# Attention and local-attention kernel: the finishing of a slot moved into the next slot's first point, more sums by transfer, more key tiles in parts

## The chip, the cores and the metric

The kernel runs on one core of one Trainium2 chip. A core has five engines with queues of their own: TensorE (PE, with its weight loads as PEld), VectorE (DVE), ScalarE (ACT), GpSimd (POOL) and SyncE (SP), which here only issues transfers. Transfers run on 16 DMA engines that all issuers share. The metric is the device time of the core in microseconds (us), as the median of several runs. A profile is one execution recorded by the hardware; its span runs from the first to the last instruction.

## The reference

Two layers work on four images of 64 x 64 pixels with 256 channels, in float32. Layer 0 is full self-attention over the 4096 pixels of an image, with a residual. Layer 1 is a depthwise 3x3 convolution with three outputs a channel, two pointwise layers with a GELU between, a residual, and attention over each pixel's 3x3 neighbours.

```python
# layer 0, x: (4, 4096, 256), q and k have 32 channels
energy = jnp.einsum('bnd,bmd->bnm', q, k)
attn = jax.nn.softmax(energy, axis=-1)
x = gamma * jnp.einsum('bnm,bmc->bnc', attn, v) + inputs
# layer 1
perceived = depthwise_conv3x3(x) + b_perc             # 768 channels
hid = gelu(w_up1 @ perceived + b_up1)                 # 512 channels
h_new = x + w_up2 @ hid + b_up2
return h_new + local_attention_3x3(h_new)             # zero-padded borders
```

## The kernel before

**Slots and points.** Layer 0 is cut into 32 slots of 512 queries (4 images, 8 slots each; slot `s` is block `s % 8` of its image). A slot goes through the 4096 keys of its image in 16 half groups of 256 keys, that is two key tiles of 128 each, counted `n` = 0 to 15 (`G, half = divmod(n, 2)`). The main loop gives one point to each half group. Layer 1 follows the slots at a distance: convolution two slots behind, hidden layer three, local attention five. Its pieces are jobs, hung on points by the lists `jobs`, so that each point has attention work and one piece of layer 1. The tile framework turns what the program says into waits, but each engine takes its instructions in the order of the program text, which is written out by hand. So an instruction that waits holds up all that stands behind it on its engine.

**One point** (main loop from L1246): SyncE issues the loads that are due (keys, values, forms); ScalarE makes the high part of the next half group's weights; TensorE does the energies of the half group after that (`energy`, L400), ScalarE their exponentials into a tile `p` (three buffers); then come the jobs of layer 1, and then `product` (L423), which adds values times weights to the accumulators. After that VectorE does `add_up` for the next half group (L480), and some tap steps of the convolution, as many as the list `share` says for this point.

**Whole and in parts.** A float32 product on TensorE can be made whole (L435, operands in float32), or in parts: the weights are split into a high part `ph` (ScalarE), a low part `pl` and a gap `pg` (VectorE, L502 and L506), the values likewise in forms kept in HBM, and three products in the reduced float32 kind (`F32R`, L458) give two sums in PSUM, which `finish` puts together. Half groups 2, 4 to 14 (`IN_PARTS`) are in parts in all slots but 0, 2 and 31. In "full" slots (25: all but 0, 1, 2, 7, 15, 23 and 31) half groups 3, 5 to 13 (`ONE_IN_PARTS`) have their second tile in parts and their first whole; `oh`, `ol`, `og` (L420, L486, L489) are the parts and `vo` (L326) the forms of that tile, in four rotating buffers `vs`. Half groups 0, 1 and 15 are whole.

**Sums of the weights.** The softmax's denominator needs the sum of all `p`. Of a full slot's half groups, 3 to 13 are sent by POOL as transfers that add (`send`, L470), the odd ones into a tile `sent`, the even ones into a tile of the pair `xc`; VectorE adds 0, 1, 2, 14 and 15 (L504) and then the two sent tiles (L513), the two halves (L514), and makes sums by 32 (`partial_sums`, L524).

**The slot's end.** `finish` (L545) stands after point 15. TensorE folds the partial sums over partitions (`dps`, L551); VectorE takes reciprocals (L554), spreads them (L540, L543), adds the two accumulators (L567) after ScalarE has scaled the gap sum (L561), scales by the reciprocal (L569) and adds the result to the image in SBUF (L575). Four accumulator banks are all there are, so product 0 of the next slot waits for L567 or L569. TensorE's other work shares two banks `m`, in turn.

**Slots with projections.** In slots 0, 7, 15 and 23 `project_v` (L334) makes the values of an image and packs them with their forms in HBM.

Of the kernel before, what the change touches and what calls it, by code (L numbers as in the profile page):

```python
# [9 lines left out]
F32 = mybir.dt.float32  # L10
F32R = mybir.dt.float32r
# [5 lines left out]
P = 128  # L17
# [35 lines left out]
ONE_IN_PARTS = (3, 5, 7, 9, 11, 13)  # L53
BY_DMA = (ONE_IN_PARTS, (4, 6, 8, 10, 12))
# [6 lines left out]
def attention_then_perception_kernel(  # L61
# [37 lines left out]
    def unshifted():  # L99
# [107 lines left out]
        queries, keys, values, forms, staged = {}, {}, {}, {}, {}  # L207
# [7 lines left out]
        packed_o = tc.dram_tile([P, NSLOT, 2, C], F32, name="packed_o")  # L215
# [10 lines left out]
        def one_in_parts(s, n):  # L226
            return full(s) and n in ONE_IN_PARTS
# [96 lines left out]
        def load_one(s, n):  # L324
            forms[s, n] = tile_of([P, NB], "vs", f"vo_{s}_{n}", 4)
            nc.sync.dma_start(  # L326
                out=forms[s, n].rearrange("p (f c) -> p f c", c=C),
                in_=packed_o[:, block(s, n // 2)],
            )
# [4 lines left out]
        def project_v(s, pair, tag="m"):  # L334
# [11 lines left out]
            split, one = n in IN_PARTS, n in ONE_IN_PARTS  # L346
            h = packed_h[:, s, bass.ts(pair, 2 * C)].rearrange("p (t c) -> p t c", c=C)
            if not split or s < NBLK or s >= NSLOT - NBLK:
# [11 lines left out]
                if not split:  # L360
                    tiles = slice(0, 1 if one else 2)
                    nc.gpsimd.dma_start(out=h[:, tiles], in_=v[:, tiles])
            if split:
                high = fresh(f"vh_{s}_{pair}")
                both = tile_of([P, 2, NB], "sent", f"vlg_{s}_{pair}")
                both = both.rearrange("p f (t c) -> p f t c", c=C)
                to = h, packed_f[:, s].rearrange("p f (t c) -> p f t c", c=C)
            elif one:
                high = fresh(f"vh_{s}_{pair}")[:, 0:1]
                both = fresh(f"vlg_{s}_{pair}").rearrange("p f (t c) -> p f t c", c=C)  # L370
                of = of[:, 1:2]
                to = h[:, 1:2], packed_o[:, s].rearrange("p f (t c) -> p f t c", c=C)
            else:
                return
            low, gap = both[:, 0], both[:, 1]
# [5 lines left out]
            for at, part in zip(to, (high, both)):  # L381
                nc.gpsimd.dma_start(out=at, in_=part)

# [10 lines left out]
        weights, highs, lows, gaps, sent = {}, {}, {}, {}, {}  # L394
        sums, accs, lsums, lrdens = {}, {}, {}, {}
        parts_, inverses, turneds = {}, {}, {}
# [20 lines left out]
        def high_one(s, n):  # L417
            high = tile_of([P, NB], "vs", f"oh_{s}_{n}", 4)
            p = weights[s, n // 2, n % 2]
            nc.scalar.activation(high.bitcast(F32R), p[:, 1, :], AF.Identity, scale=BELOW)  # L420
            highs[s, n] = high

        def product(s, G, half):  # L423
            p = weights[s, G, half]
            first = G == 0 and half == 0
            if first:
                n = 2 * CH if in_two_sums(s) else CH
                accs[s] = [bank("acc", f"acc_{s}_{c}") for c in range(n)]
            v = values[s, G][:, 2 * half : 2 * half + 2]
            last = G == NG - 1 and half == 1  # L430
            if not in_parts(s, G, half):
                one = one_in_parts(s, 2 * G + half)
                for i in range(1 if one else 2):
                    for c in range(CH):
                        nc.tensor.matmul(  # L435
                            accs[s][c], lhsT=v[:, i, bass.ts(c, P)], rhs=p[:, i, :],
                            start=(first and i == 0), stop=(last and i == 1),
                        )
                if one:
                    at = s, 2 * G + half  # L440
                    f = forms.pop(at)
                    for w, to, x in (
                        (v[:, 1], 0, highs[at]), (f[:, :C], 0, lows[at]), (f[:, C:], CH, gaps[at])
                    ):
                        for c in range(CH):
                            nc.tensor.matmul(  # L446
                                accs[s][to + c], lhsT=w[:, bass.ts(c, P)].bitcast(F32R),
                                rhs=x.bitcast(F32R), start=False, stop=False,
                            )
                return  # L450
            f = forms.pop((s, G, half))
            n = IN_PARTS.index(2 * G + half)
            for part, (w, to, x) in enumerate((
                (v, 0, highs[s, G, half]), (f[:, :2], 0, lows[s, G, half]), (f[:, 2:], CH, gaps[s, G, half])
            )):
                for i in range(2):
                    for c in range(CH):
                        nc.tensor.matmul(  # L458
                            accs[s][to + c], lhsT=w[:, i, bass.ts(c, P)].bitcast(F32R),
                            rhs=x[:, i, :].bitcast(F32R),  # L460
                            start=(to > 0 and n == 0 and i == 0),
                            stop=(to > 0 and n == len(IN_PARTS) - 1 and i == 1),
                        )

        def by_dma(s, n):
            if n in BY_DMA[1]:
                return full(s)
            return 0 < s < NSLOT - 1 and (s < 2 or s % NBLK < NBLK - 1) and n in BY_DMA[0]

        def send(s, n):  # L470
            p = weights[s, n // 2, n % 2]
            even = 1 - n % 2
            if n == BY_DMA[even][0]:
# [6 lines left out]
        def add_up(s, G, half):  # L480

            n = 2 * G + half
            if one_in_parts(s, n):
                low, gap = (tile_of([P, NB], "vs", f"o{x}_{s}_{n}", 4) for x in "lg")
                high = highs[s, n]
                nc.vector.tensor_tensor(  # L486
                    low.bitcast(F32R), weights[s, G, half][:, 1, :], high, ALU.subtract
                )
                nc.vector.scalar_tensor_tensor(  # L489
                    gap.bitcast(F32R), low, -SPLIT, high, ALU.mult, ALU.add  # L490
                )
                lows[s, n], gaps[s, n] = low, gap
            p = weights[s, G, half]
            if G == 0 and half == 0:
                sums[s] = tile_of([P, 2, NB], "den", f"den_{s}")
                return
            den = sums[s]
            before = weights[s, 0, 0] if (G, half) == (0, 1) else den
# [4 lines left out]
            if not by_dma(s, n):  # L503
                nc.vector.tensor_tensor(den, before, p, ALU.add)  # L504
# [5 lines left out]
            if G == NG - 1 and half == 1:  # L510
                for even in range(2):
                    if (s, even) in sent:
                        nc.vector.tensor_tensor(den, den, sent.pop((s, even)), ALU.add)  # L513
# [24 lines left out]
        def on_all(values, turned, out):  # L538

            nc.vector.tensor_copy(  # L540
# [3 lines left out]

        def finish(s, parts=((0, RB),)):  # L545

            acc = accs.pop(s)
# [11 lines left out]
            os = [tile_of([P, NB], "o", f"o_{s}_{c}", 2) for c in range(CH)]  # L559
            for o, gap in zip(os, acc[CH:]):  # L560
# [1241 lines left out]
```

## Time and profile before

| what | us |
|---|---|
| median of 3 runs (3247.27 to 3250.21) | 3248.11 |
| the profiled execution's own time | 3249.86 |
| its span | 3248.1 |
| PE busy / DVE busy / ACT busy / POOL busy | 3218.2 / 2866.3 / 1449.8 / 724.1 |
| a late full slot, from fold to fold | 94.4 to 95.2 |

The chain of work that ended last puts 75% of the span on PE and 17% on DVE. The 16 DMA engines moved 190 GB/s in the mean.

How to read it: a group of instructions is named by its line in the kernel, its engine and operation, and the tiles out<-in. Matmuls are pipelined and the ends of their records are modelled, so a record of 592 ns can follow the one before it after 430; what a stretch of PE costs is read from start to start. An f32 matmul has two records, one of the reduced kind has one. A wait is put down to what ended last before it. Busy time is not the same as being the limit: what counts is which wait ends last in a stretch.

### The profile page before, as it was taken

The page shows a single profiled execution, that of the slowest core. Times are in us where ns is not written, and L with a number is a line of the kernel's source. Part 1 is how long each engine was busy: PE and PEld are TensorE (multiplying, and loading weights), DVE is VectorE, ACT ScalarE, POOL GpSimd, SP SyncE. Part 2 cuts the span into 40 slices and gives each one's busy share as a digit, 9 for nine tenths or more (in the row PEclk, how much of TensorE's full clock was granted, in tenths as well). Part 3 has the DMA queues.
Part 4 walks back from the last instruction along what each step waited for, and adds up shares of the span by engine and source line. Part 5 has one row for each costly group of instructions (what it writes and reads, how often), then busy time and mean ns, then how long its engine had stood idle before and what let it go on. Part 6 is the DMA issues. An engine that isn't in the chain of part 4 may idle for free.

```text
span 3248.1 us, 37927 instructions
## 1 busy us (share of the span) xinstructions
PE 3218.2 (99%) x12286; PEld 2223.2 (68%) x12286; DVE 2866.3 (88%) x4380; ACT 1449.8 (45%) x1845; POOL 724.1 (22%) x970
## 2 busy tenths in 40 slices
PE   9999999999999999999999999999999999999998
PEld 5557767766776677676767767776677677667655
DVE  4779899898999999988999999998799999999895
ACT  4434444444444444444444444444444444444331
POOL 3201122221222221222122222211221122222021
PEclk9999999999999999999999999999999999999999
DMA  7767766777667777667766677776777666777100
GB/s 254 222 165 202 194 187 191 202 230 205 196 187 200 211 211 191 186 196 243 205 191 193 184 200 213 208 194 192 253 210 195 190 191 185 201 210 204 49 25 28
DMA packets 289964, 616.58 MB, mean 190 GB/s; under 512 B 97424, under 2 KB 98464, under 8 KB 289632
## 3 DMA queue, kind: packets, MB, share of 16 engines
q1 hardware_dynamic: 228608, 409.47, 40.5%
q0 software_dynamic: 53472, 191.17, 24.8%
q10 hardware_dynamic: 7680, 13.44, 1.1%
q8 instruction: 102, 1.67, 0.2%
q14 instruction: 102, 0.84, 0.1%
HBM read 386.24 MB, written 76.41 MB: 142 GB/s over the span
## 4 chain that ended last, share of the span: by engine, by line
PE 75%; DVE 17%; issue 3%; DMA 2%; ACT 1%; POOL 1%; SPq 0%; ACTq 0%; DVEq 0%; POOLq 0%
PE acc L435 19%; PE acc L458 11%; PE dx L836 5%; PE e L404 5%; DVE perc L666 5%; PE hid_bc L779 5%; PE hid_de L779 4%; PE hid_gf L779 4%; PE acc L446 4%; PE v L339 3%; PE lv L999 3%; PE g L932 3%; PE lo L1133 2%; PE hid_a L779 2%; DVE den L513 2%
## 5 line engine op out<-in xcount | busy, mean ns | idle before, releaser
L666 DVE SCALAR_TENSOR_TENSOR perc<-xp,wb,perc 128x526 f32<-128x526 f32 (+1 forms) x1356 | 941.2, 758 | 1.5 <-ACT perc L662 1.4
L435 PE MATMUL acc<-p,v 128*128 128x512 f32 x1872 | 854.5, 592 | 0.2 <-ACT v L355 0.2
L409 ACT ACTIVATE p<-e 128x1024 f32<-128x1024 f32 x512 | 524.3, 1024 | 546.6 <-PE e L404 490.5
L435 PEld LDWEIGHTS acc<-p,v 128*128 128x128 f32 x1872 | 351.7, 190 | 341.9 <-issue 328.2
L478 POOL DMA_DIRECT2D sent<-p x235 | 201.3, 857 | 1125.6 <-ACT p L409 948.9
L404 PE MATMUL e<-qa,ka 128*128 128x512 f32 x1024 | 368.3, 440 | 2.0 <-ACT p L409 1.1
L414 ACT ACTIVATE ph<-p 128x1024 fp32r<-128x1024 f32 x203 | 214.3, 1056 | 213.2 <-PE acc L458 131.6
L506 DVE SCALAR_TENSOR_TENSOR pg<-pl,ph 128x1024 fp32r<-128x1024 f32 x203 | 267.2, 1316 | 9.0 <-PE e L404 0.5
L502 DVE TENSOR_TENSOR pl<-p,ph 128x1024 fp32r<-128x1024 f32 x203 | 252.2, 1242 | 18.5 <-ACT ph L414 16.8
L458 PE MATMUL acc<-ph,v 128*128 128x512 f32 x812 | 264.0, 447 | 0.2 <-DMA v<-packed_h 0.2
L404 PEld LDWEIGHTS e<-qa,ka 128*128 128x128 f32 x1024 | 189.5, 189 | 88.2 <-issue 45.7
L420 ACT ACTIVATE oh<-p 128x512 fp32r<-128x512 f32 x150 | 94.5, 630 | 317.6 <-PE acc L446 265.4
L836 PE MATMUL dx<-hid,wup 128*128 128x512 f32 x512 | 229.8, 592 | 0.0
L458 PE MATMUL acc<-pl,vf 128*128 128x512 f32 x812 | 223.3, 397 | 0.0
L458 PE MATMUL acc<-pg,vf 128*128 128x512 f32 x812 | 218.7, 391 | 0.9 <-DVE pg L506 0.9
L504 DVE TENSOR_TENSOR den<-den,p 128x1024 f32<-128x1024 f32 x161 | 207.1, 1287 | 5.7 <-ACT p L409 5.3
L1088 POOL TENSOR_TENSOR lsum<-lsum,lp 128x99 f32<-128x99 f32 (+1 forms) x179 | 208.8, 1173 | 11.7
L458 PEld LDWEIGHTS acc<-ph,v 128*128 128x128 f32 x812 | 148.2, 189 | 51.3 <-issue 26.8
L458 PEld LDWEIGHTS acc<-pl,vf 128*128 128x128 f32 x812 | 152.7, 188 | 37.1
L458 PEld LDWEIGHTS acc<-pg,vf 128*128 128x128 f32 x812 | 152.5, 188 | 37.2 <-DVE pg L506 1.4
L802 ACT ACTIVATE hid<-hid,bup 128x512 f32<-128x512 f32 x120 | 80.2, 715 | 211.0 <-DVE hid L786 211.0
L672 DVE TENSOR_TENSOR perc<-perc 128x262 f32<-128x262 f32 x360 | 167.6, 486 | 6.3
(217 smaller groups left out, 4953.3 us busy)
## 6 DMA issues: line engine op xcount, KB each, us to landing
sent<-p POOLq DMA_DIRECT2D x287, 512.0 KB, 6.2
vf<-packed_f SPq DMA_DIRECT2D x203, 512.0 KB, 5.4
v<-packed_h SPq DMA_DIRECT2D x200, 512.0 KB, 4.4
ka<-packed SPq DMA_DIRECT2D x1016, 64.0 KB, 2.8
vo<-packed_o SPq DMA_DIRECT2D x150, 256.0 KB, 4.1
xp<-in_x SPq DMA_DIRECT2D x30, 528.0 KB, 6.1
packed_f<-vlg POOLq DMA_DIRECT2D x28, 512.0 KB, 4.5
xc<-in_x SPq DMA_DIRECT2D x56, 256.0 KB, 3.9
```

The source lines that it names most:

```text
L404: nc.tensor.matmul(e[:, i, :], lhsT=keys[s, G][:, bass.ts(2 * half + i, P)].bitcast(F32R), rhs=queries[s].bitcast(F32R), start=True, stop= ...
L409: nc.scalar.activation(p, e, AF.Exp)
L414: nc.scalar.activation(high.bitcast(F32R), weights[s, G, half], AF.Identity, scale=BELOW)
L435: nc.tensor.matmul(accs[s][c], lhsT=v[:, i, bass.ts(c, P)], rhs=p[:, i, :], start=(first and i == 0), stop=(last and i == 1),)
L458: nc.tensor.matmul(accs[s][to + c], lhsT=w[:, i, bass.ts(c, P)].bitcast(F32R), rhs=x[:, i, :].bitcast(F32R), start=(to > 0 and n == 0 and ...
L502: nc.vector.tensor_tensor(low.bitcast(F32R), p, high, ALU.subtract)
L504: nc.vector.tensor_tensor(den, before, p, ALU.add)
L506: nc.vector.scalar_tensor_tensor(gap.bitcast(F32R), low, -SPLIT, high, ALU.mult, ALU.add)
L666: nc.vector.scalar_tensor_tensor(acc, win, wt, acc, ALU.mult, ALU.add)
L779: nc.tensor.matmul(ps[:, n * C : (n + 1) * C], lhsT=w(j), rhs=rows_of(mixes[s, j][:, kind, :]), start=(j == 0), stop=(j == MULT - 1),)
L836: nc.tensor.matmul(ps, lhsT=wup2[:, d, bass.ts(c, P)], rhs=hids[s][:, d, :], start=(d == 0), stop=(d == NHC - 1),)
L1088: nc.gpsimd.tensor_tensor(to, to, near_ws[block, half][:, t_, of, :], ALU.add)
```

## The change

1. `finish` of a slot in two sums is split. At the slot's end only `evacuate` remains: ScalarE scales the gap sums and VectorE adds the accumulators. The fold, the reciprocal, the scaling and the residual come in the next slot's point 0, behind its jobs and ahead of its product.
2. In full slots half groups 0 to 13 are summed by transfer (2 to 13 in the first slot of an image); VectorE keeps 14 and 15 (and 0 and 1 there).
3. In full slots half groups 1 and 15 get their second tile in parts as well, and 11 and 13 get both tiles. The first tile's forms and parts lie in the four quarters of the buffer `hid`, which the hidden layer uses at points 0 to 7. `low_and_gap` does the VectorE part for each such tile.
4. Two small operations go from VectorE to ScalarE: the spreading of the local denominator's reciprocals and the first scaling of the edge terms.
5. `share` is changed.

```diff
-ONE_IN_PARTS = (3, 5, 7, 9, 11, 13)
-BY_DMA = (ONE_IN_PARTS, (4, 6, 8, 10, 12))
+ONE_IN_PARTS = (1, 3, 5, 7, 9, 11, 13, 15)
+BOTH_IN_PARTS = (11, 13)
+BY_DMA = (3, 5, 7, 9, 11, 13)
+BY_DMA_IF_FULL = tuple(range(14))
...
+        def alone(s, n):
+            return [i for i, ns in enumerate((BOTH_IN_PARTS, ONE_IN_PARTS)) if full(s) and n in ns]
...
+        def load_alone(s, n):
+            for i in alone(s, n):
+                if i:
+                    f, *rest = [tile_of([P, NB], "vs", f"vo_{s}_{n}", 4)] + [None] * 3
+                else:
+                    four = tile_of([P, NHC, NB], "hid", f"vo_{s}_{n}_0")
+                    f, *rest = (four[:, j] for j in range(NHC))
+                forms[s, n, i], rests[s, n, i] = f, rest
+                nc.sync.dma_start(
+                    out=f.rearrange("p (f c) -> p f c", c=C), in_=packed_o[:, block(s, n // 2), i]
+                )
...
+        def high_alone(s, n):
+            for i in alone(s, n):
+                high = rests[s, n, i][0]
+                if high is None:
+                    high = tile_of([P, NB], "vs", f"oh_{s}_{n}", 4)
+                p = weights[s, n // 2, n % 2][:, i, :]
+                nc.scalar.activation(high.bitcast(F32R), p, AF.Identity, scale=BELOW)
+                highs[s, n, i] = high
+
+        def low_and_gap(s, n):
+            for i in alone(s, n):
+                high, (_, low, gap) = highs[s, n, i], rests.pop((s, n, i))
+                if low is None:
+                    low, gap = (tile_of([P, NB], "vs", f"o{x}_{s}_{n}", 4) for x in "lg")
+                p = weights[s, n // 2, n % 2][:, i, :]
+                nc.vector.tensor_tensor(low.bitcast(F32R), p, high, ALU.subtract)
+                nc.vector.scalar_tensor_tensor(
+                    gap.bitcast(F32R), low, -SPLIT, high, ALU.mult, ALU.add
+                )
+                lows[s, n, i], gaps[s, n, i] = low, gap
...
+                apart = alone(s, n)
+                todo += [(v[:, i], 0, p[:, i, :], F32) for i in range(2) if i not in apart]
+                for i in apart:
+                    at = s, n, i
+                    f = forms.pop(at)
+                    todo += [
+                        (v[:, i], 0, highs[at], F32R), (f[:, :C], 0, lows[at], F32R),
+                        (f[:, C:], CH, gaps[at], F32R),
+                    ]
...
         def by_dma(s, n):
-            if n in BY_DMA[1]:
-                return full(s)
-            return 0 < s < NSLOT - 1 and (s < 2 or s % NBLK < NBLK - 1) and n in BY_DMA[0]
+            if full(s):
+                return n in BY_DMA_IF_FULL and (n > 1 or s % NBLK > 0)
+            return 0 < s < NSLOT - 1 and (s < 2 or s % NBLK < NBLK - 1) and n in BY_DMA
...
             if not by_dma(s, n):
-                nc.vector.tensor_tensor(den, before, p, ALU.add)
+                if s in sums:
+                    nc.vector.tensor_tensor(sums[s], sums[s], p, ALU.add)
+                elif s in firsts:
+                    sums[s] = tile_of([P, 2, NB], "den", f"den_{s}")
+                    nc.vector.tensor_tensor(sums[s], firsts.pop(s), p, ALU.add)
+                else:
+                    firsts[s] = p
...
+        def evacuate(s):
+            acc = accs.pop(s)
+            os = [tile_of([P, NB], "o", f"o_{s}_{c}", 2) for c in range(CH)]
+            for o, gap in zip(os, acc[CH:]):
+                nc.scalar.mul(o, gap, -1.0 / (SPLIT + 1.0))
+            if in_two_sums(s):
+                for c, o in enumerate(os):
+                    nc.vector.tensor_tensor(o, acc[c], o, ALU.add)
+                acc = os
+            evacuated[s] = os, acc
...
-            on_all(inverses[at][:, 1, :], turneds[at][:, 1, :], lrdens[s])
+            on_all(inverses[at][:, 1, :], turneds[at][:, 1, :], lrdens[s], nc.scalar.copy)
...
-                nc.vector.tensor_scalar(edge[:, to], of(0), wc[:, 0:1], None, ALU.mult)
+                nc.scalar.mul(edge[:, to], of(0), wc[:, 0:1])
...
-            share = [1, 5, 8, 6, 5, 2, 7, 4, 6, 3, 4, 2, 1, 0, 0, 0]
+            share = [2, 6, 8, 4, 7, 2, 7, 4, 6, 4, 3, 1, 0, 0, 0, 0]
...
-                if one_in_parts(slot, point + 1):
-                    load_one(slot, point + 1)
+                load_alone(slot, point + 1)
...
-                if by_dma(slot, point + 1):
-                    send(slot, point + 1)
+                at = behind[0], 2 * behind[1] + behind[2]
+                if by_dma(*at):
+                    send(*at)
...
                 for do in jobs[point]:
                     do()
+                if slot and point == 0 and in_two_sums(slot - 1):
+                    next(finish(slot - 1))
...
-            if slot < NSLOT - 1:
+            if in_two_sums(slot):
+                evacuate(slot)
+            elif slot < NSLOT - 1:
                 next(finish(slot))
```

## The prediction

> **What bounds the kernel now.** I read the page's busy table first, then the chain and the waits, then one slot's timeline and the windows by slot, and last SyncE's own timeline beside the DMA share.
>
> ```profile
> PE 3218.2 (99%) x12286; PEld 2223.2 (68%) x12286; DVE 2866.3 (88%) x4380; ACT 1449.8 (45%) x1845; POOL 724.1 (22%) x970
> ```
>
> TensorE is in use 99% of the span at a granted clock of 0.999, so what shortens its stream shortens the kernel as long as nothing makes it wait. The PE timeline of slot 10 (start, length, then engine, line, tiles) prices that stream: half group 13 with one tile whole and one in parts, and the end of the slot. The line with "x8" is from the chain: a product of two whole tiles.
>
> ```profile
> 1016.54 0.61 PE L404 MATMUL e<-qa,ka 128*128 128x512 f32 x2
> 1017.00 1.88 PE L435 MATMUL acc<-p,v 128*128 128x512 f32 x4
> 1018.31 1.03 PE L446 MATMUL acc<-oh,v 128*128 128x512 f32 x2
> 1019.18 0.63 PE L446 MATMUL acc<-ol,vo 128*128 128x512 f32 x2
> 1019.65 0.62 PE L446 MATMUL acc<-og,vo 128*128 128x512 f32 x2
> 1020.10 0.62 PE L404 MATMUL e<-qa,ka 128*128 128x512 f32 x2
> ...
> 1028.67 0.41 PE L551 MATMUL dps<-parts,fold 128*128 128x32 f32 x2 [0.85 <-DVE parts L533]
> ```
>
> ```profile
> 1044.31 3.43 PE acc L435 x8
> ```
>
> Records overlap, so I read start to start. Eight records are four f32 matmuls: 3.43/4 = 0.858 us each, 1.715 us a whole tile (two output halves). The steps 0.47 and 0.45 are pairs of reduced matmuls: 0.233 us each, 6 x 0.233 = 1.40 us a tile in parts. Check: 0.466 (energy) + 1.715 + 1.40 = 3.58 against 3.56 from energy to energy.
>
> The fold (`dps`) waits at the slot's end for VectorE. Windows cut at the fold give two kinds of slot (columns: length, then busy of PE, PEld, DVE, ACT, POOL); below them, the wait's total and count.
>
> ```profile
> 933.45:1028.67 95.22, 94.37 (x368) 67.08 (x368) 88.53 (x134) 44.13 (x54) 21.60 (x25) 1.00 0.71 196
> 1123.78:1218.31 94.53, 94.28 (x368) 67.08 (x368) 87.75 (x130) 44.08 (x54) 22.53 (x26) 1.00 0.71 198
> ```
>
> ```profile
> PE dps L551 <- DVE parts L533: 8.6, 20, 1.0
> ```
>
> VectorE is not far behind: 87.75 of 94.5 us. In slot 11 most of its idle time is at the start (2.82 before `hid_de`, 1.44 before `hid_gf`); from there to the fold it runs with gaps of some 0.035 us.
>
> ```profile
> 1041.76 0.69 DVE L786 TENSOR_TENSOR hid<-hid_de,hid 128x512 f32<-128x512 f32 x1 [2.82 <-PE hid_de L779]
> 1044.35 0.69 DVE L786 TENSOR_TENSOR hid<-hid_gf,hid 128x512 f32<-128x512 f32 x1 [1.44 <-PE hid_gf L779]
> ```
>
> Third resource: the DMA engines (window, then the last two columns, share and GB/s), and SyncE's issues at points 12 and 13.
>
> ```profile
> 939.00:945.00 6.00, 6.00 (x21) 3.76 (x20) 4.68 (x8) 1.04 (x2) 0.00 (x0) 1.00 0.02 7
> 997.00:1012.00 15.00, 15.00 (x59) 10.61 (x59) 14.82 (x21) 6.55 (x9) 3.83 (x4) 1.00 1.01 277
> 1012.00:1020.00 8.00, 8.00 (x35) 6.13 (x34) 7.85 (x10) 4.00 (x5) 5.21 (x6) 1.00 0.90 232
> ```
>
> ```profile
> 1011.28 0.32 SPq L326 DMA_DIRECT2D vo<-packed_o  x1
> 1011.65 3.39 SPq L233 DMA_DIRECT2D ka<-packed  x4
> 1015.09 0.46 SPq L312 DMA_DIRECT2D v<-packed_h  x1
> ```
>
> Early in a slot the engines are empty, from point 9 to 13 they are full. The value load at 1015.09 (group 7) lands 5.2 us later, at 1020.26; product 14 needs it at 1020.89. In eight slots (10 to 14, 18, 19, 21) this margin is 0.63, 2.0, 0.76, 1.0, 1.8, 0.89, 2.1 and 1.45 us, mean 1.33. That is the thinnest cover in the kernel.
>
> **What the Trainium skill says.** "FP8 and Floating Point Precision" (TensorE Precision Notes) gives true FP32 four passes and "TensorE: Matmul & The Clock Gate" (Wait — 56ns, not 53.3ns?) 215.7 ns for a warm 512-column matmul: 0.863 and 0.216 us; the trace has 0.858 and 0.233. "DMA: Bandwidth & Descriptors" (Issuing engines are not separate DMA queues) says DMAs of all issuers share 16 engines and interleave: here the key loads issued from 1011.65 landed around 1018, just after POOL's 512 KB sum landed. "SBUF — State Buffer" (SBUF: two separate sides) says a VectorE operation with two SBUF inputs and a GpSimd operation that reads SBUF lock each other out: `og` took 1.34 us at 1015.04 beside `lsum` on POOL, 0.722 in the mean.
>
> **The change part by part**, per full slot (25: 3–6, 8–14, 16–22, 24–30).
>
> *Parts.* Four more tiles (half groups 1, 15, and the second tile of 11, 13): 4 x (1.715 - 1.40) = 1.26 us less PE; 25 x 1.26 = **-31.5**. The PE records are the same kinds in the same places, so I take this as certain where the operands are there in time.
>
> *Fold.* It moves behind the hidden products and `lv` of the next point 0, 0.47 + 3.9 + 1.73 = 6.1 us of PE later; its wait of 8.6 us in all is then covered: **-8.6**. What takes its place: product 0 needs the accumulators, whose two sums (L567, 0.67 each) now stand right behind the partial sums; and the fold's "m" bank needs the `hid_bc` addition (0.69). By my count VectorE ends the partial sums 2.2 to 3.3 us after product 15 and the two sums 1.4 later, against 6.3 when product 0 starts: no stall, 1.6 us to spare. Scaling and residual cost the same on VectorE, 5 us, in place of the idle 2.82 and 1.44.
>
> *VectorE.* Added: four times 0.682 + 0.722 (L486, L489) = 5.62. Removed: three sums (3 x 1.287 = 3.86), the copy for `lrden` (L540, 0.424) and two edge scalings (L971, 0.45), both to ScalarE. Net +0.9: 88.6 busy of 93.0. Slots 8, 16, 24 lose one sum instead of three: near 92.5 of 93.4, so they gain little; I charge 0.7 each, **+2**. Shares move three tap steps (0.76 or 0.49 each) ahead of point 10, which pays for most of the new work at 11, 13 and 15. Adding up in order, `og` of 13's second tile comes 0.3 to 0.5 us before the PE wants it, `pg` of 14 0.3 to 1.3; the lock with POOL can take that.
>
> *ScalarE.* 4 x 0.63 + 0.6 + 0.45 = 3.6 on 44. The edge scaling waits for VectorE's `h`; behind it stand point 8's `oh` and exponential, which wait for product 7 and an energy anyway: nothing. ScalarE's new high parts at 11 and 13 stand before an exponential that is due a point later: nothing; uncovered, 0.63 each.
>
> *Sums by transfer.* 22 x 3 + 3 = 69 more issues on POOL (0.857 us) of 512 KB. The page has 24.8% of 16 engines for 191 MB: 2.2 us of all engines each. They fall at points 15 to 2, where the share is 0.02 to 0.7, and hold a `p` buffer (three) until landed, about 6 us of the three points that there are: nothing. The first waits for VectorE's last sum; behind it on POOL stands only watching.
>
> *Loads.* 100 more `vo` of 256 KB; at 40.5% for 409 MB each is 0.84 us of all 16 engines. Those of 1 and 15 have room. Those of 11 and 13 (first tile) enter SyncE's queue ahead of the keys and values of points 12 and 14, where the engines are full: 1.7 us more, of which 1012–1020 can absorb some 0.8. So group 7's values land 0.8 to 1.7 us later, I take 1.2, and are wanted 0.3 to 0.6 earlier because products 11 and 13 are shorter: 1.65. Over the eight margins max(0, 1.65 - margin) averages 0.44; at the low end (1.1) 0.14, at the high end (2.3) 0.97. With up to 0.1 for VectorE's thin places in the same stretch, which overlap: 0.5 x 22 = **+11** (3 to 24). If it were covered: 0.
>
> *Projections* (slots 0, 7, 15, 23) make more parts on engines with over 20 us idle a slot: nothing, at most +2.
>
> Sum: 3248.1 - 31.5 - 8.6 + 2 + 11 = **3221** on the profiled span. That execution took 3249.86, 1.8 around the span; the median of the runs is 3248.11, so the same difference puts the median at 3221 too.
>
> **Rivals.** (a) *Covered*: the late loads fit, as the early slots' do, and margins hold: 3248.1 - 40.1 = 3208. For it: five of eight margins are 1.0 or more, and `vo` of 11's first tile waits for no late reader, so it may go out early. Against: share 1.01. (b) *The DMA backlog takes most*: the 1.7 us add up with the keys of point 14 (1.7 us of cover, gone when products shorten) to a stall of 1 to 1.7 us: 22 x 1.35 = +30 for +11: 3240, between 3233 and 3254. (c) *VectorE becomes the bound* (slower): if its 4.3 us at `hid_de`/`hid_gf` do not shrink, because the moved finish leaves the same order of waits, each slot is the old 94.5 plus 0.9 and another 0.3 of lock, and three slots 2.6 more: 22 x 0.8 (net of the fold's slack) + 3 x 2 = +24: 3272. It decides where less than 2.7 of those 4.3 us is taken up: 88.6 busy and about 2.5 of small gaps leave 1.9 us in 93.0. Against it: at point 0 the finish now stands exactly in that hole. (d) The change doesn't do what it says: excluded for the parts, since TensorE's instructions are written out.
>
> **How the numbers follow.** Forecast 0.50 (own range 3210 to 3233), (a) 0.27, (b) 0.13, (c) 0.08, else 0.02. The range 3204 to 3241 leaves out (c) and part of (b). 0.2% is 6.5 us, about what a measurement of this kernel can tell from no change: faster is below 3241.6. Forecast, (a) and half of (b): 0.83; same 0.07; slower 0.10.
>
> **What would show it.** Full slots near 93.2 to 93.8 us from fold to fold; L551 without idle before it and `hid_de` idle on VectorE below 1 us; `acc<-p,v` from 1872 to 1472 records; new PE idle, if any, on product 14's `ph` released by a load of `v`, or by `ka` at the energy before; DMA share above 0.95 from point 9 to 13. PE idle released by VectorE (`og`, `pg`) at 12 to 14 would say that the order on VectorE is the tighter cover; a fold that still waits would prove me wrong, and so would slots of over 95 us.

## The result, and the profile after

| | before | after |
|---|---|---|
| median, us | 3247.9 | 3203.8 (3203.1 to 3205.3) |
| ratio, 95% interval | | 0.9864 (0.9846 to 0.9881) |
| span of the profiled execution, us | 3248.1 | 3201.4 |
| a late full slot other than 16 and 24, from fold to fold, us | 94.4 to 95.2 | 92.6 to 92.8 (two took 93.0 and 93.1) |

The kernel is 44 us faster; 27 were forecast. First the page's busy table of the kernel after, and the records of whole products in the groups of PE:

```profile
PE 3179.4 (99%) x12486; PEld 2261.7 (71%) x12486; DVE 2903.6 (91%) x4428; ACT 1550.8 (48%) x2068; POOL 759.6 (24%) x1055
...
L481 PE MATMUL acc<-p,v 128*128 128x512 f32 x1472 | 678.9, 596 | 0.2 <-ACT v L363 0.2
```

The whole records fell from 1872 to 1472, as they had to with 100 tiles more in parts. Next the PE timeline of slot 10 of the kernel after: half group 13 with both tiles in parts, and the fold in its new place.

```profile
1007.89 0.61 PE L418 MATMUL e<-qa,ka 128*128 128x512 f32 x2
1008.35 0.62 PE L481 MATMUL acc<-vo,v 128*128 128x512 f32 x2
1008.80 1.07 PE L481 MATMUL acc<-vo 128*128 128x512 f32 x4
1009.71 0.62 PE L481 MATMUL acc<-oh,v 128*128 128x512 f32 x2
...
1011.07 0.64 PE L418 MATMUL e<-qa,ka 128*128 128x512 f32 x2
...
1024.48 0.30 PE L576 MATMUL dps<-parts,fold 128*128 128x32 f32 x2
1024.62 3.68 PE L481 MATMUL acc<-p,v 128*128 128x512 f32 x8
```

From energy to energy the half group takes 3.18 us, where one whole tile and one in parts took 3.56. The fold waits for nothing, and what follows starts 0.14 us after it (0.25 before). The windows of the kernel after: two full slots from fold to fold, then a stretch early in slot 10, 5.3 to 11.3 us after the slot's first energy, where 939 to 945 lies in the kernel before, and the two stretches up to 1.7 us before and from there to 6.3 us after product 12's start in slot 10, which lie as the two shown of before do (length; busy of PE, PEld, DVE, ACT, POOL; granted clock; share of the DMA engines; GB/s).

```profile
931.65:1024.48 92.83, 92.83 (x378) 68.57 (x377) 89.11 (x134) 47.98 (x63) 23.66 (x28) 1.00 0.84 229
1117.19:1209.80 92.61, 92.61 (x378) 68.64 (x377) 88.78 (x132) 47.55 (x61) 24.48 (x29) 1.00 0.85 231
930.90:936.90 6.00, 6.00 (x23) 3.76 (x22) 4.94 (x12) 0.93 (x2) 1.30 (x2) 1.00 0.98 301
988.30:1003.30 15.00, 15.00 (x62) 11.32 (x61) 14.79 (x23) 7.34 (x10) 3.46 (x4) 1.00 1.02 266
1003.30:1011.30 8.00, 8.00 (x38) 6.72 (x37) 7.72 (x9) 4.45 (x6) 5.16 (x6) 1.00 0.91 261
```

PE busy equals the length of the slot: as far as the records show, TensorE never stands there. The added sums fill the early stretch of the DMA engines, which was nearly empty (share 0.98, 0.02 before). The last two stretches are as full as they were (1.01 and 0.90 before), the last with 261 GB/s in place of 232. The chain that ended last is now PE for 94% (75% before). In the waits of the kernel after (engine, what for, us in total, times, longest) little is left in the full slots:

```profile
PE acc L481 <- DVE pg L520: 2.0, 3, 0.8
...
PE e L418 <- DMA ka<-packed: 0.9, 1, 0.9
PE dps L576 <- DVE parts L548: 0.7, 1, 0.7
```

I set the starts of all energies of the two traces side by side; a point is taken from its energy to the next point's. Of the 46.7 us that the span lost, the parts bring -35.2 and the fold -15.1 in the full slots; where a slot follows one with projections another 4.4 go, which no step of the prediction had; new gaps at points 11 to 14 cost +6.1 (2.4 of it in slots 8, 16 and 24, where VectorE is late), and the rest (start, first slots, end) +1.9.

### The profile page after: what moved, and what is told of

Its sections match the earlier page's. It is cut to its first block, busy times and chain, and to the rows that moved or that the text cites. A ratio compares the mean times of both kernels' runs of the same rounds, so it can differ in the third digit from the quotient of the medians.

```text
span 3201.4 us, 39239 instructions
## 1 busy us (share of the span) xinstructions
PE 3179.4 (99%) x12486; PEld 2261.7 (71%) x12486; DVE 2903.6 (91%) x4428; ACT 1550.8 (48%) x2068; POOL 759.6 (24%) x1055
## 4 chain that ended last, share of the span: by engine, by line
PE 94%; DVE 3%; DMA 1%; issue 0%; POOL 0%; ACT 0%; SPq 0%; ACTq 0%; DVEq 0%; POOLq 0%
PE acc L481 46%; PE e L418 7%; PE dx L857 7%; PE hid_de L800 5%; PE hid_gf L800 5%; PE hid_bc L800 5%; PE lv L1020 3%; PE g L953 3%; PE lo L1154 3%; PE v L347 3%; PE s L1061 2%; PE hid_a L800 2%; DVE perc L687 1%; PE qk L272 1%; PE hid L832 1%; DMA vo<-packed_o 0%
## 5 line engine op out<-in xcount | busy, mean ns | idle before, releaser
L481 PE MATMUL acc<-p,v 128*128 128x512 f32 x1472 | 678.9, 596 | 0.2 <-ACT v L363 0.2
L500 POOL DMA_DIRECT2D sent<-p x304 | 258.0, 855 | 1353.6 <-ACT p L423 823.0
L481 PEld LDWEIGHTS acc<-p,v 128*128 128x128 f32 x1472 | 275.1, 190 | 267.9 <-issue 257.6
L418 PE MATMUL e<-qa,ka 128*128 128x512 f32 x1024 | 357.1, 430 | 5.3 <-ACT p L423 1.5
L520 DVE SCALAR_TENSOR_TENSOR pg<-pl,ph 128x1024 fp32r<-128x1024 f32 x203 | 253.3, 1248 | 11.9 <-DVE pl L510 0.5
L437 ACT ACTIVATE oh<-p 128x512 fp32r<-128x512 f32 x200 | 126.4, 632 | 248.4 <-PE acc L481 83.2
L481 PE MATMUL acc<-oh,v 128*128 128x512 f32 x400 | 184.8, 543 | 0.0
L857 PEld LDWEIGHTS dx<-hid,wup 128*128 128x128 f32 x512 | 96.7, 189 | 98.5 <-issue 93.4
```

What stands on the lines that cost most here:

```text
L418: nc.tensor.matmul(e[:, i, :], lhsT=keys[s, G][:, bass.ts(2 * half + i, P)].bitcast(F32R), rhs=queries[s].bitcast(F32R), start=True, stop= ...
L437: nc.scalar.activation(high.bitcast(F32R), p, AF.Identity, scale=BELOW)
L481: nc.tensor.matmul(accs[s][to + c], lhsT=w[:, bass.ts(c, P)].bitcast(kind), rhs=x.bitcast(kind), start=to not in started[s], stop=last,)
L500: nc.gpsimd.dma_start(out=sent[s, even], in_=p, accum_op=ALU.add)
L520: nc.vector.scalar_tensor_tensor(gap.bitcast(F32R), low, -SPLIT, high, ALU.mult, ALU.add)
L857: nc.tensor.matmul(ps, lhsT=wup2[:, d, bass.ts(c, P)], rhs=hids[s][:, d, :], start=(d == 0), stop=(d == NHC - 1),)
```

## The experiments

All are edits of the kernel after, except where the kernel before is named; its line numbers are other ones. "Before" ran beside them at 3247.5 to 3250.2 us. Intervals are of the ratio to it.

**1. The fold alone, and the fold left behind.** In the first kernel, the kernel before gets only the new place of the fold, scaling and residual; in the second, the kernel after has them back at the slot's end.

```diff
# fold_alone: in before          # fold_back: in after, the reverse
+ if slot and point == 0 and in_two_sums(slot - 1):
+     next(finish(slot - 1))
...
- if slot < NSLOT - 1:
+ if in_two_sums(slot):
+     evacuate(slot)
+ elif slot < NSLOT - 1:
      next(finish(slot))
```

> The kernel before with nothing but the finish split as in the change (accumulators emptied at the slot's end, fold, scaling and residual in the next point 0). Theory S (starts): a fold that waits costs from start to start some 0.28 us more than the idle time that its record shows, and the slots after the projections lose their waits for the shared bank too: -15 in the full slots and -4.4 at the entry to slots 8, 16 and 24, some -19, so 3229 us. Theory R (records, the prediction's count): the 8.6 us of recorded idle time and nothing else, 3239 us.

Measured: 3227.0 us, ratio 0.9934 (0.9917 to 0.9951). 21 us, not 8.6. By points, 15.6 us of it lie at the ends of full slots, 5.2 at the ends of the slots with projections.

> The changed kernel with the whole finish at the slot's end again. In the changed kernel VectorE ends the partial sums 2.0 to 4.1 us after the last product of the slot. Theory V: at the slot's end TensorE would wait for all of that, and a slot is then as long as VectorE's round, about the old 94.5 us plus 0.9 of added work, so 22 slots by 2.5 us and more: about +55, 3258 us (3240 to 3270). Theory A (the parts of the change add up): it gives back only what the move alone brought, +8.6 to +19: 3212 to 3223 us.

Measured: 3295.6 us, ratio 1.0144 (1.0127 to 1.0161): 92 us slower than the kernel after, and 47 slower than the kernel before. Its slot 10 on PE, and its first wait:

```profile
1034.15 0.62 PE L481 MATMUL acc<-og,vo 128*128 128x512 f32 x2
1037.49 0.41 PE L576 MATMUL dps<-parts,fold 128*128 128x32 f32 x2 [2.72 <-DVE parts L548]
...
PE dps L576 <- DVE parts L548: 55.7, 24, 3.9
```

With the other edits in, VectorE ends a slot so late that TensorE stands 2.5 to 2.9 us at the fold in nearly all full slots (4.0 in 8, 16 and 24), where it stood at most 1.2 before (0.16 us added to each recorded wait, see experiment 2). So this edit is worth 21 us alone and 92 among the others. In 14 full slots that stall is the loss; slots 8, 16, 18 to 20 and 24 to 28 get 4.3 to 7.0 us longer, part of it behind the fold, at the next point 0. Why stays open.

**2. Why the wait was worth more than its record.** The kernel before, with the fold reading a constant tile; everything stays where it was.

```diff
+ level = pool.tile([P, 2 * NJ], F32, tag="level", name="level")
+ nc.gpsimd.memset(level, 1.0e25)
...
- given = parts_.pop(s).rearrange("p i j -> p (i j)")[:, :n]
- nc.tensor.matmul(ps, lhsT=fold, rhs=given, start=True, stop=True)
+ parts_.pop(s)
+ nc.tensor.matmul(ps, lhsT=fold, rhs=level[:, :n], start=True, stop=True)
```

> The kernel before, with one thing other: the fold of a slot multiplies a tile that holds a constant in place of VectorE's partial sums, so the denominator is left out of the result, and the fold no longer has anything of VectorE's to wait for. Nothing is moved: inverse, scaling and residual stay at the slot's end, ahead of the next slot's hid products. Theory S (what the move of the fold brought, 21 us, is the wait for VectorE, which is longer than the idle time that the trace records ahead of the fold): 3230 us, from 3227 to 3234, and TensorE goes from the last product of a full slot to the first hid product without a gap beyond the fold's own 0.14 us. Rival R (the recorded idle, 8.6 us, is all of the wait; the rest of the 21 us came from moving scaling and residual behind the next slot's first work): 3239 us.

Measured: 3233.5 us, ratio 0.9957 (0.9940 to 0.9973). The ends of the full slots get 15.5 us shorter, slot by slot the same as with the fold moved (slot 10: 1.11 and 1.12 us). The end of slot 10 on PE, in the kernel before and in this one:

```profile
1024.22 3.59 PE L435 MATMUL acc<-p,v 128*128 128x512 f32 x8
...
1028.92 0.70 PE L404 MATMUL e<-qa,ka 128*128 128x512 f32 x2
```

```profile
1023.46 0.30 PE L554 MATMUL dps<-level,fold 128*128 128x32 f32 x2
1023.60 0.71 PE L407 MATMUL e<-qa,ka 128*128 128x512 f32 x2
```

The last record of the product starts 1.445 us ahead of the fold in the kernel before, 0.429 in this one: 1.016 us of stall, where the record says 0.85, because the modelled end of the product's last record lies 0.16 us past what TensorE needed. And after a stall the next matmul starts 0.244 us after the fold's first, in place of 0.140. Together 1.12 us for a wait recorded as 0.85. Shorter waits lose more in proportion (0.41 us of stall recorded as 0.25 in slot 12), and slot 24's stall of 0.11 has no idle time on record.

The 5.2 us at the slots with projections stay in this kernel. Its waits still have what the kernel after no longer has:

```profile
PE hid_a L782 <- ACT vh L380: 2.5, 3, 1.5
...
PE hid_bc L782 <- ACT hid L795: 1.8, 3, 0.6
```

So these 5.2 us come from moving the finishing, not from the fold's wait; which of its instructions stood in the way was not tried.

**3. The sums of half groups 0 to 2 back on VectorE.**

```diff
-BY_DMA_IF_FULL = tuple(range(14))
+BY_DMA_IF_FULL = tuple(range(3, 14))
```

> The changed kernel with half groups 0 to 2 summed by VectorE again (3 to 13 by transfer): VectorE gets 3.8 us a full slot more, 22 transfers of 512 KB by three fall away. Theory V: VectorE's 88.8 us of 92.6 with some 2.4 us of small gaps has about 1.4 us left, so the slots stretch by about 2.4 us: +50, 3254 us. Rival: its 3.8 us of idle time take all of it: 3204 us, or 1 to 2 us less because the DMA engines have less to do.

Measured: 3247.9 us, ratio 0.9998 (0.9989 to 1.0006): the whole gain is gone. The waits of PE, and a window over about a slot:

```profile
PE acc L481 <- DVE pg L520: 16.3, 24, 1.0
...
PE acc L481 <- DVE og L447: 4.3, 14, 0.3
```

```profile
1104.00:1198.00 94.00, 93.34 (x377) 68.24 (x376) 91.84 (x136) 46.96 (x61) 22.48 (x30) 1.00 0.74 206
```

VectorE, 3 us busier a slot (91.84 of 94.00), now delays products 11 and 14: by points 18.3 and 20.4 us of the 44. Early sums are paid late: VectorE has 2.2 us idle in the whole window.

**4. Parts at 11 and 13, at 1 and 15, and one more at 15.** Three kernels, each one line:

```diff
# both_back
-BOTH_IN_PARTS = (11, 13)
+BOTH_IN_PARTS = ()
# ends_back (and the gap sums end with half group 14 again)
-ONE_IN_PARTS = (1, 3, 5, 7, 9, 11, 13, 15)
+ONE_IN_PARTS = (3, 5, 7, 9, 11, 13)
# both_15
-BOTH_IN_PARTS = (11, 13)
+BOTH_IN_PARTS = (11, 13, 15)
```

> The changed kernel with half groups 11 and 13 as before, one tile whole and one in parts (two loads of 256 KB fewer in each full slot, at points 10 and 12). Theory S: each tile made whole costs 0.38 us from start to start, 25 x 0.76 = +19, and some 4 us of waits at points 11 to 14 go: 3219 us. Theory R (the prediction's terms): 25 x 0.63 = +15.8 and the 11 us charged for late loads go: 3209 us.

Measured: 3218.3 us, ratio 0.9907 (0.9891 to 0.9924), 14.5 us slower. In nearly every full slot point 11 grew by 0.37 and point 13 by 0.39 us, where my step had 0.315 for each.

> The kernel after, with half groups 1 and 15 whole again in the full slots (two full-precision tiles each, as before); 11 and 13 stay with both tiles in parts. Accounting S (what a part brings at these places is the 0.32 us and 0.33 us a slot that the trace showed at points 1 and 15, 16.3 us together, and VectorE's relief brings at most the 2.3 us of late half groups in slots 8, 16 and 24 back): 3204 + 16 - 0 to 2 = 3218 to 3220 us, and the three kinds of edits of the change (fold 21, parts at 11 and 13 14.5, these two 15) then sum to more than the 44 us that the change brought, by what VectorE's fuller queue costs. Rival R (the parts at 1 and 15 are partly paid back by VectorE, which has two more splits and an adding in a slot): 3208 to 3214 us.

Measured: 3226.5 us, ratio 0.9924 (0.9908 to 0.9941), 22.7 us slower, some 20 by the ratios, since "before" took 3250.2 beside it: outside both expectations. Points 1 and 15 grew by 0.33 and 0.32 us, 16 us in all, as expected. The rest lies at point 14, 11 us in the profiled execution, the slowest of its four:

```profile
PE acc L481 <- DMA v<-packed_h: 11.6, 20, 1.0
```

Product 14 waits for its values, though this kernel moves fewer bytes. Experiment 6 takes this up.

> The kernel after, with both tiles of half group 15 in parts in place of one. TensorE has one more product in parts of its eight in 25 slots: 25 x 0.385 = 9.6 us less. VectorE gets one more adding of 1.2 to 1.4 us in a slot, and has 3.8 us idle of 92.6. If VectorE's margin is enough and the added load at point 14 is covered: 3194 us. If VectorE, which in the slots after a projection is already late, sets the end of the slot: 3202 to 3210 us.

Measured: 3214.5 us, ratio 0.9899 (0.9882 to 0.9915), 10.7 us slower than the kernel after. TensorE waits at the fold for the bank that VectorE's addition of the hid products has to free. The wait, and a window of slot 13 from fold to fold, one of the shortest:

```profile
PE dps L576 <- DVE hid L807: 6.0, 10, 1.7
```

```profile
1211.94:1304.36 92.42, 92.42 (x379) 68.94 (x378) 89.97 (x134) 48.14 (x62) 21.90 (x28) 1.00 0.85 230
```

This slot takes 92.42 us, 0.2 less than in the kernel after and not 0.39, and many gain nothing: slots 10, 11, 18 and 19 take 92.9 to 93.2, where they took 92.7 to 92.8. In every full slot point 15 is 0.36 to 0.40 us shorter, and in many the point 0 behind it takes that back; behind the slots with projections it grows by up to 2.9 us.

**5. The transfers: one more, fewer.** The first kernel adds a load ahead of group 7's values, the second leaves 50 loads out.

```diff
# more_load
+ if point == 12 and full(slot):
+     more = tile_of([P, C], "more", f"more_{slot}")
+     nc.sync.dma_start(out=more, in_=packed_o[:, block(slot, 6), 0, 0])
# fewer_loads
+ if i:
      nc.sync.dma_start(out=f..., in_=packed_o[:, block(s, n // 2), i])
...
+ if full(s) and n in BOTH_IN_PARTS:
+     forms[s, n, 0] = forms[s, n, 1]
```

> The kernel after, with one more transfer of 128 KB into a tile of its own at point 12 of each of the 25 full slots, issued on the same queue ahead of the values of half group 14; nobody reads the tile. Theory K (after the change these values land with 0.2 us to spare in the mean and 0.04 us in many slots, so the transfers are just covered and anything more ahead of them is paid at product 14): 128 KB at 213 GB/s are 0.6 us of the transfers' time, of which 0.3 to 0.6 us a slot come to the path: 3212 to 3219 us. Rival C (the transfers are covered by more than the small margin shows, since the margin is that of a queue which is served when the product is near): 3202 to 3206 us.

Measured: 3211.2 us, ratio 0.9888 (0.9871 to 0.9904): 7.4 us for 25 loads, a little under the expected band; points 13 and 14 grew by 4.7 and 3.9 us in its profiled execution.

> The kernel after, but the first tiles of half groups 11 and 13 take the high parts of the second tiles in place of a load of their own, which leaves 50 transfers out and makes the values of these two tiles wrong. All matmuls and all of VectorE's work stay. Theory of the prediction (the transfers that the change adds cost 11 us at products 12 to 14): 3193 us. Theory K (what is paid for them is what the trace shows as new gaps at points 11 to 14 outside the slots that VectorE delays, some 4 us, and the rest is just covered): 3198 to 3202 us. Nothing from them at all: 3204 us.

Measured: 3204.6 us, ratio 0.9869 (0.9852 to 0.9885), no different from the kernel after. So these 50 loads cost nothing that the runs can tell, and one load more in each full slot does cost. Landing and need, in us after product 12's start, mean over the 25 full slots, from the traces:

| | values issued | landed | product 14 starts | margin |
|---|---|---|---|---|
| before | 0.85 | 6.20 | 7.20 | 1.00 |
| after | 1.82 | 6.67 | 6.89 | 0.22 |
| fewer_loads | 1.57 | 6.06 | 6.85 | 0.79 |
| more_load | 2.57 | 7.13 | 7.22 | 0.09 |
| ends_back | 1.77 | 7.32 | 7.40 | 0.08 |
| keys_first (experiment 6) | 1.76 | 6.99 | 7.13 | 0.14 |

The smallest margin that any slot shows is 0.04 us, at which a product that waits for its load starts.

**6. What holds the values' cover.** In the kernel whose ends are whole, the values are issued no later than in the kernel after but fly 0.7 us longer. SyncE's queue shows why. First the kernel after, slot 10 (product 12 starts at 1004.97): the values of group 7, the load for half group 15, the next keys. Then the kernel with whole ends (product 12 at 1009.90).

```profile
1006.99 0.43 SPq L315 DMA_DIRECT2D v<-packed_h  x1
1010.70 0.34 SPq L335 DMA_DIRECT2D vo<-packed_o  x1
1011.10 2.63 SPq L236 DMA_DIRECT2D ka<-packed  x4
```

```profile
1011.68 0.44 SPq L315 DMA_DIRECT2D v<-packed_h  x1
1013.48 1.69 SPq L236 DMA_DIRECT2D ka<-packed  x4
1015.29 0.35 SPq L315 DMA_DIRECT2D v<-packed_h  x1
```

The load for half group 15 waits for a buffer `vs` until 5.7 us after product 12's start, and the keys behind it wait with it. Without it the keys go out 3.6 us after product 12's start, with the next values and forms behind them, and share the engines with the values in flight. The test changes only the order of the queue:

```diff
-                load_alone(slot, point + 1)
+                if point != 14:
+                    load_alone(slot, point + 1)
...
                         spread_queries(slot + 1)
+                if point == 14:
+                    load_alone(slot, point + 1)
```

> The kernel after, with one transfer moved in SyncE's queue: at point 14 the load of half group 15's high and low forms, which waits for a buffer until product 13 is nearly done, stands behind the next keys and values in place of ahead of them. The same transfers, the same bytes. Theory G (the waiting load holds the next keys back until the values of half group 14 have nearly landed; without it the four key loads start 2.3 us earlier, as in the kernel whose half groups 1 and 15 are whole, and share the engines with those values, which land 0.6 us later than the 0.2 us of margin allow): product 14 waits 0.3 to 0.6 us in most of the 25 slots, 3209 to 3218 us. Rival N (that kernel's late values have another cause, such as a different phase of the other queues, and what stands behind the values in the queue doesn't matter to them): 3202 to 3206 us.

Measured: 3212.9 us (3210.0 to 3219.3), ratio 0.9894 (0.9878 to 0.9911), 9 us slower with the same transfers; point 14 grew by 6.7 of the 7.0 us in its profiled execution. Its slot 10 (product 12 at 1003.38) in SyncE's queue, and its first wait:

```profile
1005.35 0.43 SPq L315 DMA_DIRECT2D v<-packed_h  x1
1006.95 1.76 SPq L236 DMA_DIRECT2D ka<-packed  x4
...
PE acc L481 <- DMA v<-packed_h: 6.0, 15, 0.8
```

The values flew 5.50 us there (landed 1010.85), against 4.90 in the kernel after (landed 1011.89); over the 25 full slots the mean is 5.24 against 4.85. The windows over just these flights, of the kernel after and of this one, show the company they had in the last two columns (0.74 of the engines and 215 GB/s; 0.92 and 254):

```profile
1006.99:1011.89 4.90, 4.90 (x23) 3.58 (x21) 4.76 (x6) 2.17 (x4) 4.66 (x6) 1.00 0.74 215
```

```profile
1005.35:1010.85 5.50, 5.01 (x23) 3.58 (x22) 5.36 (x6) 2.77 (x4) 5.19 (x7) 1.00 0.92 254
```

A load that the change added, and that waits, is what keeps the values on time. Whether the keys or the values and forms behind them take most of the room was not separated.

**7. Attempts at more.** With the values ahead of the keys at every even point; with the sum of half group 14 by transfer as well; with both tiles of 15 in parts and the fold behind the first product.

```diff
# values_first: load_values(*after) ahead of load_keys(*ahead)
# sums_15 in the names: and the first tile added to p of half group 15
-BY_DMA_IF_FULL = tuple(range(14))
+BY_DMA_IF_FULL = tuple(range(15))
# later_15: both tiles of 15, and in slots that follow a full one
-                if slot and point == 0 and in_two_sums(slot - 1):   # ahead of product
+                if finishes and behind_it:                          # behind add_up
# later_15_act: and in finish
-            on_all(inverse[:, 0, :], turneds[s][:, 0, :], rden)
+            on_all(inverse[:, 0, :], turneds[s][:, 0, :], rden, copy=nc.scalar.copy)
```

> The kernel after, with the values issued ahead of the keys at every even point, on the same queue; nothing else is moved. Theory G (the values of half group 14 are issued 1.8 us after product 12 starts only because four key loads are issued ahead of them; ahead of these they land 1 us or more earlier, and the keys, wanted two points later, have room): product 14 waits nowhere, and the 2 to 4 us of gaps that the transfers still cost go: 3200 to 3203 us. Rival N (the keys are late instead, or nothing was paid there): 3203 to 3208 us.

Measured: 3232.4 us, ratio 0.9947 (0.9930 to 0.9963), 28.5 slower. The values now land 1.80 us ahead of product 14 in the mean, and the keys are late in their place, since the energy just ahead of product 14 wants them:

```profile
PE e L418 <- DMA ka<-packed: 23.1, 21, 2.5
```

> The kernel after, with both tiles of half group 15 in parts (which took 3214 us by itself), and with the fold, the scaling and the residual moved once more in the 18 slots that follow a full one without projections between: from ahead of the next slot's first product to behind it and behind the splits of half groups 0 and 1. Theory Q (with both tiles of 15 in parts TensorE waits at the fold, since the fold's accumulator bank waits for VectorE's adding of the hid products, which stands behind the slot's last sums; given 3.4 us more, it doesn't wait): the 25 parts at point 15 bring 9.6 us, less the 3 us in slots 8, 16 and 24, and what VectorE, busy 90.2 us of 92.3, then costs elsewhere: 3195 to 3203 us. Rival W (VectorE's work of a slot is what bounds, wherever the fold stands; the wait goes to the splits of later points): 3208 to 3216 us.

Measured: 3217.9 us, ratio 0.9901 (0.9884 to 0.9917), against 0.9899 without the move: the runs do not tell the two apart, and theory Q's gain did not come. The time lies 2 us above rival W's range.

> As the run before it, with one thing more: the copy that spreads the inverse over its square, 0.43 us on VectorE in every slot, is ScalarE's (0.61 us there). Theory Q (VectorE is at its edge, so 0.43 us a slot less of it shows where it still delays products): 1 to 10 us faster than the run before it, 3193 to 3201 us. Rival W': the copy is on no path that matters, within 1 us of the run before it.

Measured: 3224.4 us, ratio 0.9920 (0.9903 to 0.9936), another 6.5 slower, which neither theory had. In both, TensorE's longest wait in total is for ScalarE's exponentials, some 8 us; why stays open.

> As the run before it, with the sum of half group 14 by transfer too, so that VectorE adds 1.25 us less in each full slot. TensorE's work is that of the kernel after. If VectorE still delays products there (slots 8, 16, 24: 2.3 us) and the added transfer is covered: 3198 to 3202 us. If the added transfer of 0.5 MB takes the values' room at product 14, or the denominator waits for it at the slot's end: 3206 to 3216 us.

> The kernel after with both tiles of half group 15 in parts and with the sum of half group 14 by transfer, the queue's order as it was: VectorE's work is that of the kernel after within 0.2 us a slot, TensorE's is 9.6 us less. If VectorE alone made both tiles of 15 cost time: 3192 to 3198 us. If the transfers do it: 3204 to 3216 us.

> As the run before it, with the values ahead of the keys. If both bounds (VectorE's time and the landing at product 14) are what held the parts back, and both are lifted: 3190 to 3197 us, 5 us or more below the run before it where that one pays for transfers. If something else bounds: 3203 us or more.

Measured: 3383.0 us, ratio 1.0411 (1.0394 to 1.0429); 3425.4 us, 1.0541 (1.0523 to 1.0559); 3410.0 us, 1.0497 (1.0480 to 1.0515). All far above what was expected. In the second, the waits of DVE and of PE:

```profile
DVE den L531 <- DMA sent<-p: 185.3, 25, 9.1
```

```profile
PE e L418 <- ACT p L423: 168.7, 25, 8.4
```

The transfer of half group 14 comes last in the chain of the denominator. In slot 10 POOL issued it 10.5 us after product 12's start, in its turn behind other work, and it landed at 19.2, where VectorE's last sums are due from about 11. VectorE waits for it with all that stands behind. These three therefore do not tell apart the bounds that they were made for.

## Why the prediction was wrong, step by step

The sign held, and so did the view that TensorE's stream sets the time. Two terms failed: the fold's wait, 8.6 us where 19.5 went, and the late loads, +11 us where at most 3.7 were paid. The time came 17 us under the forecast, just below the range. Rival (a), 3208, was nearest; its sum leaves out the +2 for VectorE, and with it stands at 3210.

- *Parts, -31.5.* It is -35.2. The term was 4 x (1.715 - 1.40). The 1.40 was read in a half group that mixes a whole tile with parts; in half group 13 of the kernel after twelve reduced products take 2.72 us (1008.35 to 1011.07), 0.227 each and not 0.233, so the second tile in parts at 11 and 13 gains 0.37 and 0.39 us. The one at 1 and 15 gained 0.32 to 0.33, as predicted.
- *Fold, -8.6.* This step failed most. It took the recorded idle time as what the wait costs. Experiments 1 and 2: 15.5 in the full slots (15.1 among the other edits), since a record's modelled end hides 0.16 us of each stall and TensorE starts again 0.10 us slower after it; in the 24 full slots that stall this is nearly all of the 6.5 that the term lacked. Another 5.2 (4.4 among the other edits) went where slots with projections end, which the step left out.
- *VectorE, +2.* It held: 88.8 to 89.1 us busy in 92.6 to 92.8 (88.6 of 93.0 predicted), and 2.4 us in slots 8, 16 and 24. The idle time at `hid_de` is gone, so rival (c) did not come; experiments 1 and 3 show how near it stood. Two slips do not move the sum: in (c) it is 2.4 us of the 4.3 that had to be taken up (4.3 less 1.9), not 2.7; and the slow `og` at 1015.04 ran beside POOL's `lp` (1014.56 to 1015.83) and the clearing of `lsum`, whose sums start at 1016.37, after it.
- *Loads, +11.* This step failed too. Outside slots 8, 16 and 24 the new gaps are 3.7 us in all, and the kernel without 50 of the loads is no faster. The step had the queue right: the values are issued 0.97 us later than before (1.82 for 0.85) and wanted 0.3 earlier. It left the flight as it was, and that fell from 5.35 to 4.85 us. It missed that the load for half group 15 stands in SyncE's queue as a gate: it holds the next keys, and what follows them, from 3.6 to 5.8 us after product 12's start (means over 18 late full slots), while the values are in flight. I had named the keys of point 14 only as something to be late, not as what the values compete with. Without the gate, experiment 6, the values land at 6.99 us in place of 6.20, 0.8 later, the low end of what I had, and it costs 9 us. That the change put a gate at this place was luck: nothing in it was meant so. The eight margins were also kind ones, 1.33 in the mean; over all 25 full slots it is 1.00, which would have made the term larger still.
- *What would show it.* The fold and `hid_de` came as written; the DMA share stands at 1.02 up to product 12. The slots came at 92.6 to 92.8 and not 93.2 to 93.8, which is the parts, the fold and the loads together.

With the measured terms the sum closes: 3248.1 - 35.2 - 15.1 - 4.4 + 6.1 + 1.9 = 3201.4; the last term is what the others leave.

## What to carry to other kernels

Take the cost of a wait on TensorE from start to start against the same place without a stall, not from the recorded idle time. Before charging a new load, look at the order of its queue: what it holds back while it waits can be worth as much as what it moves. And an edit's worth depends on its company: the same move of the fold was worth 21 us alone and 92 among edits that fill VectorE.

## What the runs showed that I had not expected

- A load that waits can speed the load ahead of it: the same transfers in another order cost 9 us (0.6 us longer in flight in slot 10, 0.4 in the mean).
- A stall recorded as 0.85 us cost 1.12, and one of 0.11 left no record.
- Reduced 512-column matmuls followed each other at 0.227 us in half group 13 with both tiles in parts, and at 0.233 in one that begins with a whole tile; half group 14, all in parts, also has 0.233, and the cause was not tried.
- Up to three sums of 1.25 us on VectorE early in a slot cost 44 us in 25 slots, 1.7 a slot, and nearly all of it at points 11 and 14.
